# Feed-forward norm of a local-attention block: statistics per token on VectorE, factors spread by transposes, and a new written order

## The chip, the cores and the metric

The kernel runs on one core of one Trainium2 chip. The metric is the device time of one execution in microseconds (us), where smaller is better. The kernel before takes 2536.26 us, the median of three runs that lie between 2534.42 and 2536.99.

The core has engines that run side by side, each through its own instructions strictly in their order: TensorE (PE in the profile; its weight loads are shown as PEld), VectorE (DVE), ScalarE (ACT), GpSimd (POOL) and SyncE (SP), which issues DMA transfers. They wait for one another through semaphores. Matrix results land in the memory called PSUM; everything else lives in SBUF.

## The reference

One sequence of 2048 tokens with 128 features passes through four blocks, each added to its input: an oscillator recurrence with a gate, a mixture of eight experts, causal attention with 16 heads, and a stack of six layers of local attention and feed-forward. All is float32. The change lies in the last block, called stage 4:

```python
for i in range(6):
    x = attn_layer(shift_tokens(x), Wqkv[i], q_scale[i], k_scale[i], Wo[i]) + x
    x = ffn_layer(shift_tokens(x), ln_g[i], ln_b[i], W1[i], b1[i], W2[i], b2[i]) + x

def ffn_layer(x, g, bln, W1, b1, W2, b2):
    mu = x.mean(-1, keepdims=True)
    var = ((x - mu) ** 2).mean(-1, keepdims=True)
    xn = (x - mu) / jnp.sqrt(var + 1e-05) * g + bln
    hg = xn @ W1 + b1
    a, gate = jnp.split(hg, 2, -1)
    return a * jax.nn.gelu(gate, approximate=False) @ W2 + b2
```

`attn_layer` makes queries, keys and values for 16 heads of 64, normalises queries and keys to length one, rotates them, and lets each token see its own window of 32 and the one before. `shift_tokens` moves the second half of the features by one token. `ffn_layer` has 341 gated columns.

## The kernel before, in words

Stage 4 keeps the activations transposed: features on the 128 partitions, tokens along the free axis, in two SBUF tensors, `s4[0]` (input of a layer's attention) and `s4[1]` (after attention, input of its feed-forward). Attention works on tiles of 128 tokens: 16 tiles per layer, 96 in all. The feed-forward works on groups of four tiles (512 tokens): 24 groups in all.

The work of a tile is cut into some fifty named steps, that of a group into some twenty. A list named `steps`, written out by hand in the source, gives each step a place and a lag. A loop over `i` goes through the whole list each time and issues the step for tile `i - lag`; a group's step is issued only when `i - lag` is a multiple of four. So the list is the order in which every engine gets its instructions, and since engines don't reorder, it decides what waits behind what. One pass through the list is called an iteration below; four iterations carry four tiles and one group.

The steps that matter here, with the engine in brackets:

- `ps00`, `ps01`, `ps10`, `ps11` (PE): queries (ps0) and keys (ps1) in halves of 512 columns. `sq`, `ra`, `rb` read them: squares (ACT) and the two rotation products (DVE). `ss` (DVE) sums the squares, `rn` (POOL) takes the power -1/2, `rs` (POOL) adds the rotation products, `kn` (POOL) scales the keys. `tab` (POOL) makes the rotation table of the next tile.
- `pt1`, `pt0` (PE): eight transposes each of keys and queries; `kT`, `qT` (ACT) copy them out of PSUM; `ca` (POOL) carries the last window of keys into the next tile.
- `pv0`, `pv1` (PE): values; `vt` (ACT) copies them; `vw` (SP) spreads them over windows by 16 DMAs.
- `sc0` to `sc3` (PE): scores, in small tiles of 64 rows of the array; `sm` adds the mask, `mx` takes the row maximum (DVE), `nb` (POOL) scales it, `ex` (ACT) takes 16 exponentials, `su`, `nr` (DVE) sum and divide, `ptp` (PE) transposes, `pT` (ACT) copies.
- `po0` to `po3` (PE): weights times values, again in small 64-row tiles; `oT` (ACT) copies; `px0` to `px3` (PE, every other tile) multiply by Wo in tiles of 64 rows; `s` (DVE) adds the residual into `s4[1]`.
- the group's steps: the norm (`pm` to `xcn`), then for each of three column chunks `ph`, `ge`, `act` (PE, ACT with Gelu, DVE) and `py` (PE), and `s2` (DVE), which writes the next layer's `s4[0]`. In the last layer `st` transposes and stores the output.

The norm before works without leaving the transposed form. `pm` multiplies by a constant matrix of 1/128, which leaves the mean in every partition; `xc` subtracts it; `xsq` squares on ScalarE; `pvar` multiplies the squares by a column of 1/128, with one output column per 128 tokens; `fvar` adds epsilon and `fr` takes the power -1/2; `prb` spreads the factor over the partitions by four matrix products with the identity; `xcn` multiplies by factor and gain. The norm's bias is folded into the feed-forward's bias once a layer (`bias`, tile name `pbias`).

All matrix results of stage 4 take their place in one PSUM pool, `big`, of four buffers of two banks each. A step that needs a buffer waits until the steps that read its former content are done.

Of the kernel before, what the change touches and what calls it, by code (L numbers as in the profile page):

```python
# [11 lines left out]
F32 = mybir.dt.float32  # L12
BF16 = mybir.dt.bfloat16
I32 = mybir.dt.int32
AF = mybir.ActivationFunctionType
ALU = mybir.AluOpType
# [3 lines left out]
P = 128  # L20
T = 2048
NT = T // P
G = 4
NG = NT // G
GW = G * P
EPS = 1e-5
# [12 lines left out]
NPAIR = HEADS // 2  # L39
WIN = 32  # L40
# [53 lines left out]
class Kernel:  # L94
# [825 lines left out]
    def stage4(self, x3T, out):  # L920
        nc, tc, a = self.nc, self.tc, self.a
        with ExitStack() as ctx:
            self.pools4.append(ctx.enter_context(tc.tile_pool(name="s4w1", bufs=1)))
            const = ctx.enter_context(tc.tile_pool(name="s4c", bufs=1))
            pool = ctx.enter_context(tc.tile_pool(name="s4", bufs=2))
# [9 lines left out]
            carry = const.tile([P, 1], F32, name="carry")  # L935
# [30 lines left out]
            def big(name):  # L966
                return psum.tile([P, 2, 512], F32, name=name, tag="big")
# [108 lines left out]
            def qT(t):  # L1076
                st[t]["qT"] = work("qT", [P, NPAIR, P])
                act.copy(st[t]["qT"], st[t].pop(("pt", 0)))

            def kT(t):  # L1080
                if t % NT == 0:
                    st[t]["kT"] = pool3.tile([P, NPAIR, WIN + P], F32, name="kT")
                    gps.memset(st[t]["kT"][:, :, 0:WIN], 0.0)
                act.copy(st[t]["kT"][:, :, WIN:], st[t].pop(("pt", 1)))

            def ca(t):
                if t % NT + 1 < NT:
                    st[t + 1]["kT"] = pool3.tile([P, NPAIR, WIN + P], F32, name="kT")
                    gps.tensor_scalar_mul(st[t + 1]["kT"][:, :, 0:WIN], st[t]["kT"][:, :, P:], carry)

            def sc(t, i):
                q, k = st[t]["qT"], st[t]["kT"]
# [102 lines left out]
                        dve.tensor_tensor(new, old, x[rows], ALU.add)  # L1195


            def pm(g):
                ff[g]["x"] = s4[1][:, g % NG * GW : (g % NG + 1) * GW]
                ff[g]["pm"] = big("pm")[:, 0]  # L1200
                pe.matmul(ff[g]["pm"], lhsT=mean_w, rhs=ff[g]["x"], start=True, stop=True)

            def xc(g):
                ff[g]["xc"] = pool.tile([P, GW], F32, name="xc")
                dve.tensor_tensor(ff[g]["xc"], ff[g].pop("x"), ff[g].pop("pm"), ALU.subtract)

            def xsq(g):
                ff[g]["sq"] = pool.tile([P, GW], F32, name="xsq", tag="ff")
                act.activation(ff[g]["sq"], ff[g]["xc"], AF.Square)

            def pvar(g):
                sq = ff[g].pop("sq")
                ff[g]["var"] = big("pvar")[:, 0, 0:G]
                for j in range(G):
                    pe.matmul(
                        ff[g]["var"][:, j : j + 1], lhsT=sq[:, j * P : (j + 1) * P], rhs=mean_w[:, 0:1],
                        start=True, stop=True,
                    )

            def fvar(g):  # L1220
                ff[g]["r"] = pool.tile([P, G], F32, name="fvar")
                dve.tensor_scalar_add(ff[g]["r"], ff[g].pop("var"), EPS)

            def fr(g):
                gps.tensor_tensor(ff[g]["r"], ff[g]["r"], self.mhalf[:, 0:G], ALU.pow)

            def prb(g):
                r = ff[g].pop("r")
                ff[g]["prb"] = big("prb")[:, 0]
                for j in range(G):  # L1230
                    pe.matmul(
                        ff[g]["prb"][:, j * P : (j + 1) * P], lhsT=r[:, j : j + 1].to_broadcast([P, P]), rhs=self.ident,
                        start=True, stop=True,
                    )


            def xcn(g):
                x = ff[g]["xc"]
                dve.scalar_tensor_tensor(x, x, vec[:, g // NG, 0:1], ff[g].pop("prb"), ALU.mult, ALU.mult)

            def bias(l):
                w1, vc = self.w4[l][1], vec[:, l]
# [77 lines left out]
            for n in range(4):  # L1320
                for name, f in dict(sc=sc, po=po, px=px).items():
                    tiles[f"{name}{n}"] = of(f, n)
            groups = dict(pm=pm, xc=xc, xsq=xsq, pvar=pvar, fvar=fvar, fr=fr, prb=prb, xcn=xcn, s2=s2, st=store)
            for n in range(3):
                for name, f in dict(ge=ge, act=gated, py=py).items():
                    groups[f"{name}{n}"] = of(f, n)
# [3 lines left out]


            steps = [
                ("ps00", 0), ("po1", 4), ("fr", 10), ("po2", 4), ("ss1", 1), ("pt1", 2), ("ps01", 0), ("po3", 4),
                ("ss0", 1), ("kT", 2), ("s2", 15), ("sq0", 0), ("pv0", 2), ("oT", 4), ("pv1", 2), ("su", 3),
                ("sc0", 2), ("ra0", 0), ("rb0", 0), ("vt", 2), ("sc1", 2), ("sc2", 2), ("ph10", 11), ("ge0", 13),
                ("ph20", 13), ("pt0", 1), ("sc3", 2), ("ph11", 11), ("rs1", 1), ("vw", 2), ("py0", 14),
                ("act0", 13), ("qT", 1), ("nr", 3), ("sm", 2), ("mx", 2), ("rn", 1), ("ph21", 13), ("xsq", 9),
                ("ps10", 0), ("ge1", 11), ("ps11", 0), ("ptp", 3), ("py1", 14), ("st", 15), ("ph00", 12), ("nb", 2),
                ("sq1", 0), ("px0", 4), ("ge2", 13), ("ph01", 12), ("px1", 4), ("act1", 11), ("kn", 1), ("pT", 3),
                ("prb", 10), ("py2", 14), ("ra1", 0), ("px2", 4), ("px3", 4), ("pm", 8), ("ex", 2), ("act2", 13),  # L1340
                ("pvar", 9), ("ca", 2), ("rb1", 0), ("xc", 8), ("xcn", 10), ("fvar", 9), ("s", 4), ("tab", -1),
                ("po0", 3), ("rs0", 0),
            ]
            last = DEPTH * NT
            self.wo4 = {}
# [114 lines left out]
```

## Time and profile before

| | us |
|---|---|
| median of three runs | 2536.26 |
| the profiled execution's own time | 2534.71 |
| its span, first to last instruction | 2533.0 |
| PE busy in the span | 2423.0 (96%) |
| DVE busy | 1844.1 (73%) |
| ACT busy | 1728.4 (68%) |
| POOL busy | 1471.4 (58%) |
| stage 4, from its first `ps` at 846.25 to the end | 1687 |

Busy time is the union of an engine's instructions. The groups of the profile name what an instruction writes and reads (`sc<-kT,qT`), its shape, how many there were, their busy time together and the mean duration of one, and then the idle time of the engine before them with what ended it. Durations of matrix instructions overlap, so what one costs on PE is read from the timeline, as the distance between the starts of two runs. In the timeline a line is a run of equal instructions: start, length, engine, what it does, and how many. Every float32 matrix product appears as two instructions, a transpose as one. All stage 4 instructions carry line 66, a helper's, so they are told apart by the tensors' names. Rows written `SP` and `SPq` are the DMA issuing engine.

### The profile page before, as it was taken

The page shows a single profiled execution, that of the slowest core. Times are in us where ns is not written, and L with a number is a line of the kernel's source. Part 1 is how long each engine was busy: PE and PEld are TensorE (multiplying, and loading weights), DVE is VectorE, ACT ScalarE, POOL GpSimd, SP SyncE. Part 2 cuts the span into 40 slices and gives each one's busy share as a digit, 9 for nine tenths or more (in the row PEclk, how much of TensorE's full clock was granted, in tenths as well). Part 3 has the DMA queues.
Part 4 walks back from the last instruction along what each step waited for, and adds up shares of the span by engine and source line. Part 5 has one row for each costly group of instructions (what it writes and reads, how often), then busy time and mean ns, then how long its engine had stood idle before and what let it go on. Part 6 is the DMA issues. An engine that isn't in the chain of part 4 may idle for free.

```text
span 2533.0 us, 87720 instructions
## 1 busy us (share of the span) xinstructions
PE 2423.0 (96%) x38312; PEld 1441.2 (57%) x38312; DVE 1844.1 (73%) x2519; ACT 1728.4 (68%) x3233; POOL 1471.4 (58%) x1007
## 2 busy tenths in 40 slices
PE   5689999999999799999999999999999999999997
PEld 3663333333334466666666666666666666666665
DVE  7667765467653488887888778877888778878874
ACT  3323455634556377887888878887888788888884
POOL 3210000100001699888888878887888888888880
PEclk8889999989999899999999999999999999999999
DMA  2000000000000422233223322242223322222221
GB/s 79 1 1 1 1 1 1 1 1 2 1 1 1 103 70 71 68 90 77 70 70 78 93 62 70 66 101 66 72 67 91 76 70 70 67 60 64 65 68 38
DMA packets 100157, 130.13 MB, mean 51 GB/s; under 512 B 26553, under 2 KB 47681, under 8 KB 99777
## 3 DMA queue, kind: packets, MB, share of 16 engines
q1 hardware_dynamic: 99196, 124.07, 19.8%
q8 instruction: 304, 4.98, 0.9%
q14 instruction: 77, 0.62, 0.1%
q10 hardware_dynamic: 580, 0.46, 0.1%
HBM read 23.50 MB, written 1.05 MB: 10 GB/s over the span
## 4 chain that ended last, share of the span: by engine, by line
PE 90%; DVE 4%; ACT 3%; POOL 1%; issue 1%; DMA 0%; ACTq 0%; DVEq 0%; POOLq 0%
PE sc L66 21%; PE ps L66 14%; PE po L66 9%; PE pt L66 7%; PE pv L66 7%; PE px L66 7%; PE av L66 6%; PE ph L66 5%; PE py L66 4%; PE ptp L66 3%; PE prb L66 1%; PE pvar L66 1%; PE pm L66 1%; ACT ex L66 1%; DVE kT L66 1%
## 5 line engine op out<-in xcount | busy, mean ns | idle before, releaser
L66 POOL TENSOR_TENSOR rn<-ss,mhalf 128x32 f32<-128x32 f32 x96 | 524.2, 5460 | 8.0
L66 ACT ACTIVATE sm<-sm,mx,rn 128x64 f32<-128x64 f32 x1536 | 519.8, 429 | 3.7 <-POOL mx L66 3.0
L66 DVE TENSOR_REDUCE mx<-sc 128x1 f32<-128x512 f32 (+3 forms) x640 | 353.5, 604 | 222.3 <-PE sc L66 220.9
L66 ACT ACTIVATE ex<-sc 128x512 f32<-128x512 f32 (+3 forms) x640 | 306.1, 537 | 281.5 <-PE sc L66 280.4
L66 POOL TENSOR_TENSOR rot_a<-rot_a,rot_b 128x1024 f32<-128x1024 f32 x192 | 449.9, 2361 | 5.7 <-DVE rot_b L66 5.7
L66 PE MATMUL sc<-kT,qT 64*32 64x64 f32 (+2 forms) x13568 | 442.0, 259 | 8.6 <-ACT qT L66 7.8
L66 PE MATMUL ps<-wqkv,s 128*128 128x512 f32 x768 | 395.3, 619 | 2.0 <-DVE s L66 1.6
L66 POOL TENSOR_SCALAR_AFFINE_SELECT ex<-ex 128x512 f32<-128x512 f32 x64 | 40.6, 635 | 576.0 <-ACT ex L66 560.2
L66 PE MATMUL sc<-qT,kT 32*128 32x512 f32 (+3 forms) x1280 | 339.1, 581 | 4.0 <-DVE qT L66 2.1
L66 DVE TENSOR_TENSOR rot_a<-ps,tab 128x1024 f32<-128x1024 f32 x192 | 234.8, 1223 | 127.1 <-ACT sq L66 122.0
L66 PEld LDWEIGHTS sc<-kT,qT 64*32 64x32 f32 (+1 forms) x13568 | 219.5, 113 | 188.6 <-issue 108.7
L66 PEld LDWEIGHTS po<-pT,vw 64*64 64x64 f32 x12288 | 210.5, 135 | 184.9 <-issue 175.6
L66 ACT ACTIVATE sq<-ps 128x1024 f32<-128x1024 f32 x192 | 196.5, 1023 | 134.3 <-PE ps L66 97.1
L66 PE MATMUL po<-pT,vw 64*64 64x32 f32 x12288 | 242.1, 222 | 4.6 <-ACT pT L66 4.2
L66 DVE TENSOR_TENSOR rot_b<-ps,tab 128x1024 f32<-128x1024 f32 x192 | 232.9, 1213 | 0.0
L66 DVE TENSOR_REDUCE ss<-sq 128x16 f32<-128x1024 f32 x192 | 224.6, 1211 | 1.1
L66 PE MATMUL pt<-ident,rot_a 128*128 128x128 f32 x1536 | 211.4, 281 | 11.6 <-POOL rot_a L66 11.5
L66 PEld LDWEIGHTS pt<-ident,rot_a 128*128 128x128 f32 x1536 | 170.8, 142 | 46.4 <-issue 23.7
L66 PE MATMUL pv<-wqkv,s 128*128 128x512 f32 x384 | 190.6, 619 | 0.0
L66 PE MATMUL px<-oT,wo 64*128 64x128 f32 x3072 | 185.8, 276 | 0.8 <-DVE ot L66 0.8
L66 POOL TENSOR_TENSOR rot_a<-rot_a,rn 128x1024 f32<-128x1024 f32 x96 | 182.6, 1902 | 0.1
L66 PEld LDWEIGHTS px<-oT,wo 64*128 64x128 f32 x3072 | 176.6, 189 | 9.0 <-issue 4.5
(212 smaller groups left out, 3481.8 us busy)
## 6 DMA issues: line engine op xcount, KB each, us to landing
vw<-vt SPq DMA_DIRECT2D x1524, 64.0 KB, 2.0
wqkv<-in_L_ffn_Wqkv SPq DMA_DIRECT2D x18, 512.0 KB, 5.5
wo<-in_L_ffn_Wo SPq DMA_DIRECT2D x24, 256.0 KB, 6.0
w<-in_L_ffn_W SPq DMA_DIRECT2D x6, 341.0 KB, 3.6
x<-in_L_attn_hidden_states SPq DMA_DIRECT2D x4, 256.0 KB
out<-ot SPq DMA_DIRECT2D x4, 256.0 KB, 2.3
rot<-in_rot SPq DMA_DIRECT2D x1, 960.0 KB
w<-in_L_ffn_W SPq DMA_DIRECT2D x12, 64.0 KB, 4.9
```

What stands on the lines that cost most here:

```text
L66: return self._tc.keep_in_program_order(call(*args, **kw))
```

## The change

The norm of the feed-forward is computed another way, and the list `steps` is replaced by another one.

The new norm: `xt` transposes the group's 512 tokens of `s4[1]` by four transposes into PSUM, so that tokens lie on the partitions. `xs` lets VectorE take mean and variance of each token (for each 128 tokens a statistics instruction and one that aggregates it) and adds epsilon. `fr` on GpSimd takes the power -1/2 and makes minus mean times factor. `prb` spreads both over the partitions by eight transposes of broadcast columns. `xcn` computes x times gain times factor, and adds gain times the second row, in two VectorE instructions; `xc` is now written there. `pm`, `xc`, `xsq`, `pvar` and `fvar` are gone as steps.

The new list has other places and lags for nearly all steps. `kT`'s tile is now allocated through a helper, `keys`, by whichever of `ca` and `kT` comes first.

```diff
--- before.py
+++ after.py
@@ -1077,16 +1077,20 @@
                 st[t]["qT"] = work("qT", [P, NPAIR, P])
                 act.copy(st[t]["qT"], st[t].pop(("pt", 0)))
 
+
+            def keys(t):
+                if "kT" not in st[t]:
+                    st[t]["kT"] = pool3.tile([P, NPAIR, WIN + P], F32, name="kT")
+                return st[t]["kT"]
+
             def kT(t):
                 if t % NT == 0:
-                    st[t]["kT"] = pool3.tile([P, NPAIR, WIN + P], F32, name="kT")
-                    gps.memset(st[t]["kT"][:, :, 0:WIN], 0.0)
-                act.copy(st[t]["kT"][:, :, WIN:], st[t].pop(("pt", 1)))
+                    gps.memset(keys(t)[:, :, 0:WIN], 0.0)
+                act.copy(keys(t)[:, :, WIN:], st[t].pop(("pt", 1)))
 
             def ca(t):
                 if t % NT + 1 < NT:
-                    st[t + 1]["kT"] = pool3.tile([P, NPAIR, WIN + P], F32, name="kT")
-                    gps.tensor_scalar_mul(st[t + 1]["kT"][:, :, 0:WIN], st[t]["kT"][:, :, P:], carry)
+                    gps.tensor_scalar_mul(keys(t + 1)[:, :, 0:WIN], st[t]["kT"][:, :, P:], carry)
 
             def sc(t, i):
                 q, k = st[t]["qT"], st[t]["kT"]
@@ -1195,48 +1199,45 @@
                         dve.tensor_tensor(new, old, x[rows], ALU.add)
 
 
-            def pm(g):
+
+            def xt(g):
                 ff[g]["x"] = s4[1][:, g % NG * GW : (g % NG + 1) * GW]
-                ff[g]["pm"] = big("pm")[:, 0]
-                pe.matmul(ff[g]["pm"], lhsT=mean_w, rhs=ff[g]["x"], start=True, stop=True)
-
-            def xc(g):
-                ff[g]["xc"] = pool.tile([P, GW], F32, name="xc")
-                dve.tensor_tensor(ff[g]["xc"], ff[g].pop("x"), ff[g].pop("pm"), ALU.subtract)
-
-            def xsq(g):
-                ff[g]["sq"] = pool.tile([P, GW], F32, name="xsq", tag="ff")
-                act.activation(ff[g]["sq"], ff[g]["xc"], AF.Square)
-
-            def pvar(g):
-                sq = ff[g].pop("sq")
-                ff[g]["var"] = big("pvar")[:, 0, 0:G]
+                ff[g]["xt"] = big("xt")[:, 0]
                 for j in range(G):
-                    pe.matmul(
-                        ff[g]["var"][:, j : j + 1], lhsT=sq[:, j * P : (j + 1) * P], rhs=mean_w[:, 0:1],
-                        start=True, stop=True,
-                    )
-
-            def fvar(g):
-                ff[g]["r"] = pool.tile([P, G], F32, name="fvar")
-                dve.tensor_scalar_add(ff[g]["r"], ff[g].pop("var"), EPS)
+                    cols = slice(j * P, (j + 1) * P)
+                    pe.transpose(ff[g]["xt"][:, cols], ff[g]["x"][:, cols], self.ident)
+
+            def xs(g):
+                x = ff[g].pop("xt")
+                mv = ff[g]["mv"] = pool.tile([P, G, 2], F32, name="fmv")
+                for j in range(G):
+                    sx = pool.tile([P, 6], F32, name="fst")
+                    dve.bn_stats(sx, x[:, j * P : (j + 1) * P])
+                    dve.bn_aggr(mv[:, j, :], sx)
+                dve.tensor_scalar_add(mv[:, :, 1], mv[:, :, 1], EPS)
 
             def fr(g):
-                gps.tensor_tensor(ff[g]["r"], ff[g]["r"], self.mhalf[:, 0:G], ALU.pow)
+                mv, r = ff[g].pop("mv"), pool.tile([P, 2, G], F32, name="fvar")
+                gps.tensor_tensor(r[:, 0], mv[:, :, 1], self.mhalf[:, 0:G], ALU.pow)
+                gps.tensor_scalar_mul(r[:, 1], mv[:, :, 0], -1.0)
+                gps.tensor_tensor(r[:, 1], r[:, 1], r[:, 0], ALU.mult)
+                ff[g]["r"] = r
 
             def prb(g):
                 r = ff[g].pop("r")
-                ff[g]["prb"] = big("prb")[:, 0]
-                for j in range(G):
-                    pe.matmul(
-                        ff[g]["prb"][:, j * P : (j + 1) * P], lhsT=r[:, j : j + 1].to_broadcast([P, P]), rhs=self.ident,
-                        start=True, stop=True,
-                    )
+                ff[g]["prb"] = big("prb")
+                for i in range(2):
+                    for j in range(G):
+                        pe.transpose(
+                            ff[g]["prb"][:, i, j * P : (j + 1) * P], r[:, i, j : j + 1].to_broadcast([P, P]), self.ident
+                        )
 
 
             def xcn(g):
-                x = ff[g]["xc"]
-                dve.scalar_tensor_tensor(x, x, vec[:, g // NG, 0:1], ff[g].pop("prb"), ALU.mult, ALU.mult)
+                x = ff[g]["xc"] = pool.tile([P, GW], F32, name="xc")
+                p_, by = ff[g].pop("prb"), vec[:, g // NG, 0:1]
+                dve.scalar_tensor_tensor(x, ff[g].pop("x"), by, p_[:, 0], ALU.mult, ALU.mult)
+                dve.scalar_tensor_tensor(x, p_[:, 1], by, x, ALU.mult, ALU.add)
 
             def bias(l):
                 w1, vc = self.w4[l][1], vec[:, l]
@@ -1320,7 +1321,7 @@
             for n in range(4):
                 for name, f in dict(sc=sc, po=po, px=px).items():
                     tiles[f"{name}{n}"] = of(f, n)
-            groups = dict(pm=pm, xc=xc, xsq=xsq, pvar=pvar, fvar=fvar, fr=fr, prb=prb, xcn=xcn, s2=s2, st=store)
+            groups = dict(xt=xt, xs=xs, fr=fr, prb=prb, xcn=xcn, s2=s2, st=store)
             for n in range(3):
                 for name, f in dict(ge=ge, act=gated, py=py).items():
                     groups[f"{name}{n}"] = of(f, n)
@@ -1330,16 +1331,15 @@
 
 
             steps = [
-                ("ps00", 0), ("po1", 4), ("fr", 10), ("po2", 4), ("ss1", 1), ("pt1", 2), ("ps01", 0), ("po3", 4),
-                ("ss0", 1), ("kT", 2), ("s2", 15), ("sq0", 0), ("pv0", 2), ("oT", 4), ("pv1", 2), ("su", 3),
-                ("sc0", 2), ("ra0", 0), ("rb0", 0), ("vt", 2), ("sc1", 2), ("sc2", 2), ("ph10", 11), ("ge0", 13),
-                ("ph20", 13), ("pt0", 1), ("sc3", 2), ("ph11", 11), ("rs1", 1), ("vw", 2), ("py0", 14),
-                ("act0", 13), ("qT", 1), ("nr", 3), ("sm", 2), ("mx", 2), ("rn", 1), ("ph21", 13), ("xsq", 9),
-                ("ps10", 0), ("ge1", 11), ("ps11", 0), ("ptp", 3), ("py1", 14), ("st", 15), ("ph00", 12), ("nb", 2),
-                ("sq1", 0), ("px0", 4), ("ge2", 13), ("ph01", 12), ("px1", 4), ("act1", 11), ("kn", 1), ("pT", 3),
-                ("prb", 10), ("py2", 14), ("ra1", 0), ("px2", 4), ("px3", 4), ("pm", 8), ("ex", 2), ("act2", 13),
-                ("pvar", 9), ("ca", 2), ("rb1", 0), ("xc", 8), ("xcn", 10), ("fvar", 9), ("s", 4), ("tab", -1),
-                ("po0", 3), ("rs0", 0),
+                ("ps00", 0), ("pT", 4), ("ps01", 0), ("ph21", 14), ("mx", 3), ("py0", 15), ("xcn", 11), ("rn", 2),
+                ("py1", 15), ("nb", 3), ("py2", 15), ("sq0", 0), ("ra1", 1), ("po0", 4), ("po1", 4), ("ge2", 14),
+                ("ex", 3), ("rb1", 1), ("rb0", 0), ("po2", 4), ("kn", 2), ("s2", 15), ("tab", -1), ("px0", 5),
+                ("px1", 5), ("st", 15), ("px2", 5), ("ra0", 0), ("ph00", 13), ("xt", 9), ("act2", 14), ("xs", 9),
+                ("ss1", 1), ("px3", 5), ("po3", 4), ("s", 5), ("pt1", 2), ("kT", 2), ("vw", 3), ("ph10", 11),
+                ("ph01", 13), ("pt0", 1), ("ph11", 11), ("ca", 3), ("ss0", 1), ("oT", 4), ("pv0", 2), ("qT", 1),
+                ("pv1", 2), ("su", 3), ("sc0", 2), ("rs1", 1), ("sc1", 2), ("nr", 3), ("vt", 2), ("sc2", 2),
+                ("sc3", 2), ("ge1", 11), ("ge0", 13), ("sm", 2), ("ps10", 0), ("act0", 13), ("ps11", 0),
+                ("prb", 10), ("fr", 9), ("act1", 11), ("ph20", 13), ("ptp", 3), ("sq1", 0), ("rs0", 0),
             ]
             last = DEPTH * NT
             self.wo4 = {}
```

## The prediction

> **What bounds the kernel now.** I read the page first, then busy time by stretches of stage 4, then the waits, then the order of matrix instructions.
>
> ```profile
> PE 2423.0 (96%) x38312; PEld 1441.2 (57%) x38312; DVE 1844.1 (73%) x2519; ACT 1728.4 (68%) x3233; POOL 1471.4 (58%) x1007
> ...
> PE 90%; DVE 4%; ACT 3%; POOL 1%; issue 1%; DMA 0%; ACTq 0%; DVEq 0%; POOLq 0%
> ```
>
> PE makes up 90% of the chain that ended last. By stretches (length; PE, PEld, DVE, ACT, POOL busy; granted clock; DMA share, GB/s):
>
> ```profile
> 1400.00:1700.00 300.00, 300.00 (x5804) 195.93 (x5804) 241.53 (x251) 242.13 (x430) 250.65 (x148) 0.99 0.30 74
> ...
> 1464.00:1471.00 7.00, 7.00 (x77) 4.27 (x76) 3.67 (x6) 2.78 (x7) 6.92 (x5) 0.53 0.01 2
> ```
>
> In 300 us PE has no gap; DVE, ACT and POOL are free for a sixth of it. The second row is a stretch at half clock, used below. The waits of 860 to 2480 us say the same:
>
> ```profile
> POOL mx L66 <- DVE mx L66: 215.4, 81, 5.6
> ...
> PE pt L66 <- POOL rot_a L66: 8.8, 2, 4.9
> ```
>
> The others wait often; PE's longest sum is 8.8 us. The starts of `pm` confirm it: most groups follow each other at exactly 67.77 us. So stage 4 costs what its PE instructions cost, and that is read from the timeline (start, length, run):
>
> ```profile
> 1600.97 1.05 PE L66 MATMUL pvar<-mean_w,xsq 128*128 128x1 f32 x8
> 1601.95 0.67 PE L66 MATMUL po<-pT,vw 64*64 64x32 f32 x32
> 1602.55 1.12 PE L66 MATMUL ps<-wqkv,s 128*128 128x512 f32 x2
> 1603.60 1.14 PE L66 MATMUL po<-pT,vw 64*64 64x32 f32 x64
> 1604.67 1.09 PE L66 MATMUL pt<-ident,rot_a 128*128 128x128 f32 x8
> 1605.60 1.02 PE L66 MATMUL ps<-wqkv,s 128*128 128x512 f32 x2
> 1606.55 0.67 PE L66 MATMUL po<-pT,vw 64*64 64x32 f32 x32
> 1607.15 1.98 PE L66 MATMUL pv<-wqkv,s 128*128 128x512 f32 x4
> 1609.07 1.17 PE L66 MATMUL sc<-kT,qT 64*32 64x64 f32 x96
> 1610.17 1.09 PE L66 MATMUL pt<-ident,rot_a 128*128 128x128 f32 x8
> 1611.19 0.45 PE L66 MATMUL sc<-kT,qT 64*32 64x64 f32 x32
> 1611.57 1.13 PE L66 MATMUL py<-act,w 128*128 128x512 f32 x2
> 1612.54 1.88 PE L66 MATMUL ps<-wqkv,s 128*128 128x512 f32 x4
> 1614.25 1.04 PE L66 MATMUL ptp<-ident,sm 128*128 128x128 f32 x8
> ```
>
> A run costs the distance to the next start. Four `ps` among full-size runs cost 1.71, so 0.43 each; four `pv` between `po` and `sc` cost 1.92. A visit to the small 64-row tiles thus delays the full run before it by 0.09 and the one after it by 0.10 (single starts show which). The visit pays a third part: 64 `po` cost 1.07, 32 cost 0.60, so 0.13 to 0.14 is fixed. One visit costs **0.33**, or 0.29 where transposes follow (late by 0.06). The 0.11 of one transpose is eight `ptp` in 0.87.
>
> **The change on PE, per group of four iterations.** *Work removed:* `pm` 0.95, `pvar` 0.98, old `prb` 0.89, together 2.82. *Added:* `xt`, four transposes giving way to `po`, 3 x 0.11 + 0.20 = 0.53; new `prb`, eight, 0.88. Net -1.4.
>
> *Visits removed:* before, each iteration goes to `po` three times and `sc` twice; with the one `px` run that `pvar` parts from `po` that is 21. After, `sc` is whole (4 visits), and `po` with `px` is one block in iterations 0, 2 and 3 and two in iteration 1 (counting iterations by i modulo 4): 9. Twelve fewer at 0.31 are 3.7. Against it speaks the Trainium skill, "TensorEngine Tiling (Array Packing)", Key Properties: changing the tiling mode, not just the tile, drains TensorE; the new order goes from `po` (64*64) to `px` (64*128) and back inside a block, in iterations 0 and 2. By the rule all four changes cost. The nearest row: `px` gives way to `po` 0.10 late; `po` to `px` is nowhere in the trace, bounded by 0 and the 0.14 with which `po` gives way to full runs. I take the upper: 4 changes 0.48 against 0.10 before, so -3.7 becomes -3.3. Were they free, another 0.5 would go.
>
> Laid end to end in the new order with these costs, PE needs 15.35, 14.79, 17.08 and 15.74 in iterations 0 to 3, together **63.0**, against 67.8 (-1.4 and -3.3 agree).
>
> **The other engines, and the waits.** Their sums per group: DVE 55.9 today from its groups; `xc` (0.69) goes, a second product (0.74) comes, and `xs` comes for `fvar` (0.16). The groups of the first 860 us, before stage 4, have the same statistics (busy, mean ns | idle before):
>
> ```profile
> L66 DVE BATCH_NORM_STATS2 ln_st<-x 128x6 f32<-128x128 f32 x48 | 12.7, 265 | 0.0
> ...
> L66 DVE BATCH_NORM_AGGREGATE ln_mv<-ln_st 128x2 f32<-128x6 f32 x48 | 8.7, 182 | 1.7
> ```
>
> Pairs start 0.39 apart there, so `xs` costs 4 x 0.39 + 0.3 = 1.9, DVE 57.7. There the source is SBUF, here PSUM: the mask addition reads PSUM in 1.22 and the division SBUF in 1.22, so I take no surcharge (bounds 0 and twice, 1.0). ACT loses `xsq` (0.63); four table loads of 1.28 stay, as the Gelu steps again touch two spells between exponentials. POOL: 57.0 plus `fr` 1.04 + two small operations of 0.2. All stay under 63, but with 5 to 9 to spare, so order decides. I walked the new order through one cycle by hand, with the durations above, ACT copies 0.92 apart, 16 exponentials 5.42, `rn` 5.46, `rs` 2.36, 0.1 to 0.2 per hand-over, and the built program's buffer waits:
>
> - *Iteration 1.* The second half of `ps` ends at 1.8; `sq0` runs 2.0 to 2.95, the exponentials to 8.4, `kT` to 9.4. PE is through `po`, `ph00`, `xt`, `pt1` (5.4, just held by `ra0`, 5.5), `ph01` and `pt0` at 8.1. `pv0` takes the buffer that `kT` empties: it waits until 9.45, **1.4**. Behind it stand `pv`, `sc`, `ps1`, `ptp` and the next tile.
> - *Iterations 0 and 2* pay a table load, so `kT` ends at 10.7 and 11.3, but there `pv0` takes `px`'s buffer (free once `s` has read it, 8.1 and 8.9, wanted 9.5 and 10.4), and `sc` starts at 11.3 and 12.2. No wait. The nearest miss: `ps10` wants `qT`'s buffer at 12.66, free at 12.65.
> - *Iteration 3*: `py` comes early, `pv0` is wanted at 9.9 and `kT` done at 9.4. `s2` (6.0) and `xcn` precede `ph10` (7.3). No wait.
> - *DVE*: `mx` of an iteration ends between -0.8 and +1.0 about its start, before `nb` is wanted at 2.9. `xs` ends at 7.3 in iteration 1; its cover is the wait for `kT`: 0.4 more for each statistics instruction would delay `pt0` to where PE notices.
> - *POOL*: `kn` ends by 5.0 at the latest, `pt1` wants it at 5.4 to 8.6; `tab` now waits for `rb1` (2.8), behind it `ca` (done by 5.5; `sc0` wants it at 9.9 or later), `rs1`, `fr`, `rs0`, which `pt0` wants an iteration later.
> - *SP*: `vw` issues 16 DMAs, 0.63 apart (10.2), landing 2.0 later. Released by `vt` at 12 to 14, they are in by 9.5 of the next iteration; `po` wants them at 1.8 of the one after, and the loads of the next layer stand behind them as before. Cost nothing.
>
> So a group takes 63.0 + 1.4 = **64.4**, 3.4 less. Steady stage 4 runs from 899 to 2467, 23 groups: **-79**. Filling and draining keep their number of iterations; I take nothing.
>
> *Clock.* The half-clock row shown above comes right after `pvar`, 32 `po` and `pbias` (2.3 us of one-column products in 2.9). Two of five such crossings fell to half clock; those groups took 72.1 where the others took 69.0, so 3.1 each. Without `pvar` one-column work halves: 0 to 6 us gained, I take 3. Could the new 1.4 wait bring such drops? The Trainium skill, "TensorE: Matmul & The Clock Gate", HAM oscillation, asks only that idle gaps stay below about 3.4 us: by it, no cost. The row shows a drop with no PE gap at all; at its rate, 2 in 5, 23 waits would cost 28. I go by the rule, because `pvar` alone, 1.0 of thin work in each group, never did it.
>
> Sum: 2534.7 (profiled time) - 79 - 3 = 2453; the median stood 1.6 above the profiled execution: **2455**.
>
> **Rivals.**
> - *No wait at `pv0`* (the exponentials earlier, or buffers falling otherwise): 4.8 a group, all 6 of the clock: 2536 - 110 - 6 = 2420. Against: the chain `ps01` to `kT` is fixed by rows.
> - *The fewer visits don't pay*: they come back as waits, `pv0` waiting for `kT` everywhere: iteration 0 then takes 16.6, 1 16.2, 2 18.0, 3 15.7, 66.5 in all, and only the removed work's 1.3 to 1.4 remain: 2536 - 32 = 2504. For it: margins of 0.0 to 0.5 in several places.
> - *Slower by the clock*: each group's wait at `pv0`, amid transposes, brings half-clock stretches. At 3.1 each, 1.1 per group eat the 3.4; two per group give 2455 + 143 = 2598, 1.2 or 1.3 about 2540 to 2550. For it: drops without a gap. Against: 1.4 is short.
> - *Nothing moves*: PE's gain is lost wholly to waits not seen here, 2536.
>
> **How the numbers follow.** Likeliest 2455, chance 0.55, its own range 2436 to 2476 (0.5 a group either way for the unknown change `po` to `px` and the tight margins, the clock's 0 to 6). No wait 0.10, visits not paid 0.20, nothing moves 0.05, slower 0.10. From the no-wait case to just past the unpaid visits, 2418 to 2508, leaves out about 0.15. A difference of 0.2% is about what a measurement of this kernel can tell. Faster 0.85, same 0.05, slower 0.10.
>
> **What would show it.** Groups of 64.4 (distance of `xt` starts); `sc` as runs of 128 instructions at 1.35; idle PE time before `pv`, some 1.4 once per group, ended by ACT `kT`; `xs` pairs 0.39 apart; granted clock near 1.00. Wrong: waits of PE on `pt`, `ps` or `po` in each iteration, `po` to `px` dearer than 0.14, or clock drops in every group.

## The result, and the profile after

The changed kernel takes 2513.43 us, the median of four runs between 2507.70 and 2516.99. Beside it the kernel before took 2536.01. The ratio is 0.9909, with a 95% interval of 0.9890 to 0.9929. The prediction was 2455, with a range of 2418 to 2508: the direction was right, the size was not, and the time lies just above the range.

On the page of the changed kernel, busy time and chain of work:

```profile
PE 2352.1 (94%) x38168; PEld 1445.5 (58%) x38168; DVE 1880.5 (75%) x2711; ACT 1710.1 (68%) x3209; POOL 1488.0 (59%) x1055
...
PE 86%; DVE 4%; ACT 4%; issue 2%; POOL 2%; SPq 1%; DMA 0%; ACTq 0%; DVEq 0%; POOLq 0%
```

TensorE lost 71 us of busy time (2423.0 before), close to the 79 that I forecast for the groups. But the span only fell by 20, from 2533.0 to 2513.0. So most of the work went away, and holes came in its place. The waits of 860 to 2480 us on TensorE (what it was about to do, what ended the wait; us in total, times, longest) show which:

```profile
PE sc L66 <- issue: 16.7, 15, 2.7
PE po L66 <- issue: 11.3, 9, 1.6
PE pt L66 <- POOL rot_a L66: 10.8, 3, 7.0
PE pv L66 <- ACT kT L66: 10.1, 17, 0.7
PE px L66 <- issue: 3.6, 6, 1.2
```

Before, the longest sum here was 8.8 us. Three of the five rows say "issue": TensorE stood still, although the profile shows no engine and no transfer for which it waited. The timeline shows where (start, length, run; in brackets the idle time before it):

```profile
1504.05 1.92 PE L66 MATMUL po<-pT,vw 64*64 64x32 f32 x92
1507.57 0.31 PE L66 MATMUL po<-pT,vw 64*64 64x32 f32 x4 [1.60 <-issue]
...
1577.51 1.98 PE L66 MATMUL pv<-wqkv,s 128*128 128x512 f32 x4 [0.61 <-ACT kT L66]
...
1628.96 1.20 PE L66 MATMUL sc<-kT,qT 64*32 64x64 f32 x101
1631.67 0.44 PE L66 MATMUL sc<-kT,qT 64*32 64x64 f32 x27 [1.50 <-issue]
```

A run of 96 `po` stops after 92 for 1.6 us, a run of 128 `sc` after 101 for 1.5 us. (These numbers count matrix instructions, two for each float32 product. Where I or an expectation speak of 96 or 128 products, these instructions are meant.) In the middle of a run of equal instructions nothing new is needed, so this is hardly a wait for data. I call these stops **pauses**: 0.3 us or more from the start of one instruction to the start of the next within one run of `sc`, `po` or `px`, counted from 980 to 2430 us. The kernel before has none. The kernel after has 28, which together last 33 us.

They have one thing in common. If TensorE's instructions (weight loads, products and its semaphore instructions) are numbered from the start of the trace, there are 77,540, or 302.9 times 256. The page of after lists the transfers that bring instructions in the row `q8 instruction: 303, 4.96, 0.8%`: 303 packets of 16,384 bytes, one for each 256. In the kernel after 25 of the 28 pauses stand at instruction 193 of a block of 256, whatever runs there. (The other three lie between 2420 and 2425, at a granted clock of 0.67 for the stretch 2418 to 2426.) Each of the 25 ends 1.2 to 1.6 us after a packet has landed: in block k + 1 of the program it is the k-th packet on record. The same limit holds where nothing stops. In all 3177 blocks from 980 to 2430 us of this document's fourteen kernels, no instruction 193 starts less than 1.19 us after the landing of that packet. In the kernel before 6 of 225 blocks come within 1.65 us of it, in the kernel after 36 of 228. So in a pause TensorE waits for its own program.

Groups follow each other (distance of `xt` starts) at 64.2 at the least and 66.45 in the median, where 67.77 was the rule before. The mean over the 22 whole groups fell from 68.15 to 66.91.

### The profile page after: what moved, and what is told of

Its sections match the earlier page's. It is cut to its first block, busy times and chain, and to the rows that moved or that the text cites. A ratio compares the mean times of both kernels' runs of the same rounds, so it can differ in the third digit from the quotient of the medians.

```text
span 2513.0 us, 87693 instructions
## 1 busy us (share of the span) xinstructions
PE 2352.1 (94%) x38168; PEld 1445.5 (58%) x38168; DVE 1880.5 (75%) x2711; ACT 1710.1 (68%) x3209; POOL 1488.0 (59%) x1055
## 3 DMA queue, kind: packets, MB, share of 16 engines
q8 instruction: 303, 4.96, 0.8%
## 4 chain that ended last, share of the span: by engine, by line
PE 86%; DVE 4%; ACT 4%; issue 2%; POOL 2%; SPq 1%; DMA 0%; ACTq 0%; DVEq 0%; POOLq 0%
PE sc L66 21%; PE ps L66 13%; PE po L66 9%; PE px L66 8%; PE pv L66 6%; PE pt L66 6%; PE av L66 6%; PE ph L66 5%; PE py L66 4%; PE ptp L66 3%; SPq L66 1%; PE prb L66 1%; ACT sm L66 1%; POOL rot_a L66 1%; ACT ex L66 1%
## 5 line engine op out<-in xcount | busy, mean ns | idle before, releaser
L66 PE MATMUL sc<-kT,qT 64*32 64x64 f32 (+2 forms) x13568 | 430.2, 259 | 28.3 <-issue 16.7
L66 PE MATMUL ps<-wqkv,s 128*128 128x512 f32 x768 | 373.4, 610 | 4.6 <-DVE vec L66 2.4
L66 ACT ACTIVATE sq<-ps 128x1024 f32<-128x1024 f32 x192 | 196.7, 1024 | 212.2 <-issue 109.5
L66 PE MATMUL po<-pT,vw 64*64 64x32 f32 x12288 | 235.6, 221 | 14.7 <-issue 11.3
L66 DVE TENSOR_TENSOR rot_a<-ps,tab 128x1024 f32<-128x1024 f32 x192 | 233.7, 1217 | 14.4 <-ACT sq L66 13.7
L66 PE MATMUL pt<-ident,rot_a 128*128 128x128 f32 x1536 | 200.2, 280 | 13.8 <-POOL rot_a L66 13.5
L66 PEld LDWEIGHTS ps<-wqkv,s 128*128 128x128 f32 x768 | 132.1, 192 | 109.0 <-issue 96.7
L66 PE MATMUL pv<-wqkv,s 128*128 128x512 f32 x384 | 183.7, 601 | 10.2 <-ACT kT L66 10.1
```

What stands on the lines that cost most here:

```text
L66: return self._tc.keep_in_program_order(call(*args, **kw))
```

## The experiments

All kernels with their median time, the ratio to the kernel before that ran with them, the time of the one execution that was profiled, and the mean group and the pauses (number, us together) in it. The profiled execution can lie up to 11 us from the median, so groups, pauses and waits belong with its time:

| kernel | us | ratio (95%) | profiled | mean group | pauses |
|---|---|---|---|---|---|
| before | 2536.01 | | 2534.71 | 68.15 | 0 |
| after | 2513.43 | 0.9909 (0.9890 to 0.9929) | 2514.68 | 66.91 | 28, 33 |
| v1_norm_only | 2511.61 | 0.9897 (0.9873 to 0.9920) | 2510.03 | 66.99 | 1, 0.4 |
| v2_order_only | 2562.85 | 1.0087 (1.0060 to 1.0113) | 2565.61 | 69.12 | 29, 37 |
| v3_sc_whole | 2558.15 | 1.0071 (1.0040 to 1.0102) | 2558.15 | 69.14 | 7, 6 |
| v9_sc_whole_ptp | 2632.96 | 1.0372 (1.0336 to 1.0407) | 2626.63 | 71.80 | 12, 16 |
| v5_pT_early | 2500.83 | 0.9844 (0.9816 to 0.9872) | 2491.38 | 66.10 | 24, 22 |
| v8_sc_parted | 2541.35 | 1.0023 (1.0002 to 1.0044) | 2551.58 | 68.05 | 14, 15 |
| v12_vw_once | 2493.62 | 0.9814 (0.9771 to 0.9856) | 2499.68 | 65.87 | 14, 19 |
| v13_vw_unread | 2492.35 | 0.9825 (0.9795 to 0.9855) | 2494.05 | 66.05 | 15, 21 |
| v10_po_joined | 2501.57 | 0.9859 (0.9818 to 0.9900) | 2498.23 | 66.50 | 3, 1 |
| v11_po_px_joined | 2507.77 | 0.9877 (0.9836 to 0.9918) | 2508.32 | 66.59 | 3, 3 |
| v14_po_all | 2533.39 | 0.9981 (0.9958 to 1.0004) | 2533.32 | 67.98 | 20, 25 |
| v15_po_joined_eps | 2491.03 | 0.9815 (0.9787 to 0.9843) | 2479.66 | 65.86 | 4, 4 |

### The two halves of the change

`v1_norm_only` is the new norm in the old written order:

```diff
-("pm", 8) ... ("xsq", 9) ... ("xc", 8) ... ("pvar", 9) ... ("fvar", 9)
+("xt", 8) ... ("xs", 8)          # all other places as before
```

> The new norm in the old order: xt, xs stand where pm and xc stood; xsq, pvar, fvar are gone; all else as before. Theory A (instruction supply: whole runs of small tiles outrun the delivery of PE's instructions) and the prediction's sum agree here: the old order has no whole runs, PE stays gapless, so the removed work counts in full, 1.4 us a group, 23 groups, -32: about 2504. Rival (the norm itself is what disappoints, through VectorE or PSUM buffers): no better than the changed kernel, 2513 or more.

Measured: 2511.61 beside 2538.76 for the kernel before in the same batch, 27 less. The norm's -1.4 per group times 23 were 32. So this part of the sum is nearly right, and it alone is as fast as the whole change. The most frequent group fell by 1.04, from 67.77 to 66.73: the work that went is the forecast 1.4, and most of the difference came back in the iteration with `xt`, where `pv` starts 0.10 later and `pt0` another 0.23.

`v2_order_only` is the old norm in the new order:

```diff
-("xt", 9) ... ("xs", 9) ... ("fr", 9)
+("pm", 9) ... ("xc", 9) ... ("vt", 2), ("xsq", 9) ... ("pvar", 9), ("ptp", 3), ("fvar", 9) ... ("nb", 3), ("fr", 10)
```

> The old norm in the new order: pm where xt stood, xc where xs stood, xsq behind vt, pvar ahead of ptp, fvar behind ptp, fr an iteration later behind nb. The prediction's sum: visits -3.3 and wait +1.4 leave -1.9 a group: 2536 - 44 = 2492. Theory A: pauses in whole runs (1.5 a group), po's late start (0.6), the wait at pv0 (0.6) and the end of the stage take nearly all: changed kernel plus 32, so 2540 to 2548.

Measured: 2562.85, 24 us **slower** than before, and slower than both expectations. Its waits on TensorE:

```profile
PE sc L66 <- issue: 18.0, 14, 2.3
PE po L66 <- issue: 10.5, 7, 2.1
...
PE px L66 <- issue: 4.8, 5, 1.5
```

The pauses came with the order, not with the norm: 37 us of them, and 33 in the kernel after. The forecast gives this half 44 us of gain (1.9 in each of 23 groups), and the pauses alone take most of it. Its trace also has 41 us at half clock between 960 and 2480, where the kernel before has 14; at the 3.1 us that the prediction read from each 6.8 of them, the 27 more are an estimated 12 us of loss. The rest was not followed up.

### Joining `sc` alone, in the old order

`v3_sc_whole` is the kernel before with all 128 `sc` products together:

```diff
-("sc2", 2), ("ph10", 11), ("ge0", 13), ("ph20", 13), ("pt0", 1), ("sc3", 2), ("ph11", 11)
+("sc2", 2), ("sc3", 2), ("ph10", 11), ("ge0", 13), ("ph20", 13), ("pt0", 1), ("ph11", 11)
```

> The kernel before with one edit: sc3 moved up behind sc2, so that the scores are one run of 128 matrix instructions; pt0 (and ph10, ph20 where they come) follow it. One visit of 0.33 fewer per tile. The prediction's price: -0.33 x 92 = -30, 2506, and no gap inside sc. Theory A: pauses of about 1.3 inside sc, near its end, in one tile of six, as in the changed kernel (19 us in all), none before: net -8 to -14, 2522 to 2528.

Measured: 2558.15, 19 us slower, where both theories had it faster. The saving itself is there: in an iteration without `ph`, from the start of `sc` to the start of `ptp` (`sc`, `pt`, `ps`), TensorE needs 4.06 us instead of 4.33. But its waits have a new first row:

```profile
PE ps L66 <- ACT qT L66: 18.7, 64, 0.3
...
PE sc L66 <- issue: 4.6, 7, 1.7
```

`ps` takes the PSUM buffer that `qT` empties. `qT` copies what `pt0` has transposed, and `pt0` now stands behind 32 more `sc` products. So everything from `pt0` to the next `ps` moved back by a third of a microsecond, and in three iterations of four the visit's gain of 0.27 was lost and as much again paid.

`v9_sc_whole_ptp` asks whether the visit is worth its price once that wait is covered:

```diff
# v3_sc_whole, and:
-("ps10", 0), ("ge1", 11), ("ps11", 0), ("ptp", 3)
+("ptp", 3), ("ps10", 0), ("ge1", 11), ("ps11", 0)
```

> v3_sc_whole (the kernel before with sc3 directly behind sc2; 2558), with the transposes ptp moved from behind the second ps1 product run to ahead of the first, so that the copy qT has 0.9 us more before ps1 takes its buffer. If the visit was worth its 0.3 and v3 lost only by that wait: the wait of ps for qT (62 times, 18.1 us) is gone, 92 visits at 0.29 are 27 saved, some 6 of pauses inside sc stay: 2538 - 27 + 6 = 2517. If a whole sc costs by itself, because what it holds up is released later: 2550 to 2560 with another wait in the place of qT's.

Measured: 2632.96, much slower than any expectation, and 98 us slower than the kernel before in its batch. The wait for `qT` is gone, and a larger one stands in its place, which holds half of that:

```profile
PE ptp L66 <- DVE sm L66: 48.7, 42, 1.9
PE sc L66 <- issue: 12.9, 11, 2.2
```

`ptp` needs VectorE's division of the former tile, which isn't ready that early; behind `ptp` stand both `ps1`. So the test says nothing on the price of a visit. It says that the old order had no slack there. The other half of the loss was not assigned.

### `po`'s slow start

In the kernel after, 96 `po` take 1.86 us where they follow `ps` (iterations 0 and 1), and 1.53 where they follow `ph`. The 0.33 lies in the 8th to 15th instruction, where the waits for `vw`'s DMAs stand: 0.03 to 0.076 each in the median, where the same places take 0.007 (every fourth 0.038) in v5_pT_early below. `pT`, which `po` also needs, is done 0.5 us before `po` starts. `v5_pT_early` takes that last condition away by doing `ptp` and `pT` some microseconds sooner, ahead of the second half of `ps1`:

```diff
-("ps00", 0), ("pT", 4), ("ps01", 0)
-("ps10", 0), ("act0", 13), ("ps11", 0) ... ("ph20", 13), ("ptp", 3), ("sq1", 0)
+("ps00", 0), ("ps01", 0)
+("ps10", 0), ("act0", 13), ("ptp", 3), ("pT", 3), ("ps11", 0) ... ("ph20", 13), ("sq1", 0)
```

> The changed kernel with ptp moved between ps10 and ps11, and pT behind it at the end of the iteration (lag 3), so that pT is done 1 us earlier against po0. Theory B (po's start is slow because PE reaches its waits for pT and for vw only when pT is just done): the 0.3 at po's start in iterations 0 and 1 goes, 0.6 a group, -13: about 2500. If po's slow start has another cause: no change, 2513.

Measured: 2500.83, as expected, and 96 `po` behind `ps` take 1.53 in the median. Shown next to each other, the run of after and one of this kernel:

```profile
1570.13 1.91 PE L66 MATMUL po<-pT,vw 64*64 64x32 f32 x96
```

```profile
1559.72 1.60 PE L66 MATMUL po<-pT,vw 64*64 64x32 f32 x96
```

So the cause of the slow start is shown. That the whole time fits so well is in part luck: the pauses shrank too (24, 22 us instead of 28, 33), and a new small wait of 12.9 us came, `pt` for VectorE's `rot_a`, 25 times.

### What the pauses depend on

My theory was that a dense run eats its 256 instructions faster than the next packet comes. `v8_sc_parted` breaks the run of `sc` in two:

```diff
# v5_pT_early, and:
-("pv0", 2), ("qT", 1), ("pv1", 2), ("su", 3), ("sc0", 2), ("rs1", 1), ("sc1", 2), ("nr", 3), ("vt", 2), ("sc2", 2)
+("pv0", 2), ("qT", 1), ("su", 3), ("sc0", 2), ("rs1", 1), ("sc1", 2), ("nr", 3), ("pv1", 2), ("vt", 2), ("sc2", 2)
```

> v5_pT_early (2500.8 us), with the second half of pv moved between sc1 and sc2, so that no more than 64 score products stand together. Supply theory (a packet of 256 TensorE instructions is asked for late and is there 2.3 to 2.9 us later; a whole sc run eats 256 instructions in 1.4): the runs of v5 that stand still inside sc (11 times, 14.4 us) nearly vanish, none over 0.6; one more visit to the small tiles in each of 92 iterations costs 0.29 each, +27; sum 2500.8 + 27 - 11 = 2517. If the pauses have nothing to do with how dense the run is, they stay at 14 us and the time is 2528. If a visit costs nothing in this order, only the pauses go: 2490.

Measured: 2541.35. The waits of v8_sc_parted on TensorE:

```profile
PE ps L66 <- ACT vt L66: 11.6, 37, 0.3
PE sc L66 <- issue: 9.8, 9, 2.5
PE sc L66 <- ACT kT L66: 7.9, 15, 2.1
```

The pauses in `sc` fell only from 14.4 to 9.8 us, with single ones of up to 2.5, though no run is longer than 64. So the length of the run is **not** what decides alone, and the theory fell in that form. (The pauses in `po` and `px`, whose runs weren't touched, fell from 13 to 6.) The time also went past every expectation. A new wait of 11.6 us, of `ps` for the buffer that `vt` empties later now, is part of it; the rest was not assigned.

All of its 14 pauses are at instruction 193 of a block again. Over all kernels it is 167 of 174. So the packet must be there by a fixed place, and the question becomes when it sets out. Numbering from the start of the block with its own number (the k-th packet, the k-th block), a packet starts to move at instruction 220 in the median before, and 193 of the following block (449 in the same count) is the place where TensorE stops. In the kernel after the median is 267, so packets start 47 instructions later, and 182 are left to the stop instead of 229. The medians go with the pauses: 217 to 238 in the kernels with 0 to 7 pauses, 239 to 267 in those with 14 and more, so the two ranges touch; only v9_sc_whole_ptp has 12 at 232.

What makes packets start late? `v12_vw_once` and `v13_vw_unread` ask for the transfers of `vw`. In the first they are left out for 15 tiles of 16; in the second they run into a tile that isn't read.

```diff
# v12_vw_once: the kernel after, and in vw(t)
+if t % NT:
+    st[t]["vw"] = st[t - 1]["vw"]
+    return
# v13_vw_unread: the kernel after, and in vw(t)
+if t % NT:
+    vw = const.tile([P, NWIN, NPAIR, HD], F32, name="vwd")
+    st[t]["vw"] = st[t - 1]["vw"]
+else:
+    vw = st[t]["vw"] = const.tile([P, NWIN, NPAIR, HD], F32, name="vwl")
```

> The kernel after, but vw is spread only for the first tile of each layer and all 16 tiles of the layer use it (15 of 16 tiles' values are left out): 16 DMAs per iteration and the waits of po for them go, the order of TensorE's instructions stays. It asks why instruction packets come late in the new order. If they are held up by vw's transfers, or TensorE's own look-ahead is by the many DMA waits at po: the 33 to 36 us of pauses fall below 8 and po's slow start (14 us) goes, 2513 - 28 - 14 = 2471. If the pauses belong to the order of the instructions alone: they stay near 30 us, only po's start goes, 2499. If po's slow start isn't vw's waits either: 2510.

> The kernel after; vw's 16 DMAs per iteration run as they do there, but into a tile that nobody reads, and po reads the tile of the layer's first 128 tokens (the values of the other 15 tiles are left out). The traffic stays, po's waits for it go. v12_vw_once, without both, took 2493.6 and had 14 pauses of 18.9 us, only 2 of them in po and px, where the kernel after has 15 there. If the traffic held up the instruction packets: 25 to 30 pauses again, some 12 of them in po and px, 33 us, time 2505 to 2510. If the waits did, by keeping TensorE from looking ahead: about 14 pauses as in v12_vw_once, and 2490 to 2497. In both cases po's slow start (96 po in 1.86 instead of 1.53) is gone.

Measured: 2493.62 and 2492.35, with 14 pauses of 19 us and 15 of 21 us. The first lies between its expectations, the second is the one in which the waits are behind the pauses. The waits of v13_vw_unread:

```profile
PE pv L66 <- ACT kT L66: 20.8, 22, 1.7
PE sc L66 <- issue: 17.0, 14, 2.1
...
PE po L66 <- issue: 4.3, 2, 2.4
...
PE px L66 <- issue: 0.8, 1, 0.8
```

Without `po`'s waits for the DMAs, the 16 pauses in `po` and `px` of the kernel after (three of them at half clock) became 2, and the slow start of `po` is gone (1.53 everywhere). Since it makes no difference whether the transfers run, it is the waits and not the traffic. How the waits delay the packets is not shown. It is not by the slow start: v5_pT_early has none and still 13 pauses in `po` and `px`. (Without the waits TensorE also has 720 instructions fewer, 0.9%, so the blocks' borders fall elsewhere.) The pauses in `sc` stayed at 12 and 13. Some 11 us of what was freed went into the wait of `pv` for `kT`, which grew from 10.1 to 20.8.

### Fewer visits to the small tiles, with the new norm

`v10_po_joined` joins 96 `po` in the old order:

```diff
# v1_norm_only, and:
-("ps00", 0), ("po1", 4), ("fr", 10), ("po2", 4), ("ss1", 1)
+("po1", 4), ("fr", 10), ("po2", 4), ("ps00", 0), ("ss1", 1)
```

> v1_norm_only (the new norm in the old order; 2511.6 us), with the first half of ps0 moved from between po0 and po1 to behind po2: 96 po products stand together, one visit to the small tiles fewer in each iteration. By the visits' price: -0.31 x 92 = -28, 2483. By the supply theory: 192 instructions in 1.5 us lie at the limit, a few short pauses inside po, no more than 5 us: 2483 to 2489. If visits saved come back as waits as in v3_sc_whole: 2505 to 2535, with a wait of TensorE of 0.3 or more in most iterations.

Measured: 2501.57, 10 less than v1_norm_only instead of 28, with three pauses. The most frequent group fell from 66.73 to 66.11, by half of the price of four visits. The price itself is right: from the first `po` of an iteration to `po3`, with the same work between, TensorE needs 4.31 us instead of 4.60. The other half is in the waits, 14.8 us in 22 groups:

```profile
PE pt L66 <- DVE rot_b L66: 8.2, 20, 0.7
PE pv L66 <- ACT kT L66: 6.6, 21, 0.4
```

`v11_po_px_joined` was to take three more visits per group:

```diff
# v10_po_joined, and:
-("px0", 4) ... ("ph01", 12), ("px1", 4) ... ("prb", 10), ("py2", 14) ... ("px3", 4), ("xt", 8)
+("ph01", 12), ("py2", 14), ("prb", 10), ("xt", 8), ("px0", 4) ... ("px1", 4) ... ("px3", 4)
```

> v10_po_joined, and in addition ph01, py2, prb and xt moved ahead of px, so that px and po are one block: three visits fewer per group, 3 x 0.31 x 23 = 21. By price v10's time less 21, 2462 if v10 gives 2483; by the supply theory the block px, po0 to po2 takes 320 instructions in 5.4 us, the last 192 in 1.5, so pauses no more than in v10. If the saving comes back as waits: no faster than v10.

Measured: 2507.77, with groups of 66.1 as in v10_po_joined. The expectation was mistaken: in the timeline of v10_po_joined `px` already stands as one run of 64 with `po` behind it. It is issued every second iteration, and the four steps come in the others. There was no visit to save, so this run mostly shows how far two kernels of the same TensorE work differ here, 6 us, which is within the noise of four runs each.

`v14_po_all` puts the last 32 `po` beside the other 96:

```diff
# v10_po_joined, and:
-("po2", 4), ("ps00", 0), ("ss1", 1), ("pt1", 2), ("ps01", 0), ("po3", 4)
+("po2", 4), ("po3", 4), ("ps00", 0), ("ss1", 1), ("pt1", 2), ("ps01", 0)
```

> v10_po_joined (2501.6 us; the new norm in the old order with ps00 behind po2), with po3 moved up beside po2, so that all 128 po products stand together: one visit to the small tiles fewer in each iteration. By the visits' price: -0.31 x 92 = -28, 2473. As in v10_po_joined, where half of the price came back as waits of pv for kT and of pt for rot_b: 2487. If it all comes back, or the run of 256 instructions pauses often: 2500 or more.

Measured: 2533.39, 32 us slower than v10_po_joined; the last of the three expectations came true:

```profile
PE po L66 <- issue: 13.7, 10, 1.8
PE pv L66 <- DVE s L66: 9.3, 18, 0.5
...
PE sc L66 <- issue: 8.3, 10, 2.0
```

Twenty pauses came back, 11 of them in `sc`, although `sc` stands as in v10_po_joined, which had two there. Stops at instruction 193 in other runs (`pt`, `ph`, `ps`), which my count leaves out, add 11.5 us here. So a pause needn't lie in the run that was joined.

`v15_po_joined_eps` takes on the wait for `rot_b`. In v10_po_joined one small instruction is out of proportion (GpSimd's timeline, and VectorE's beside it):

```profile
1431.50 4.68 POOL L66 TENSOR_TENSOR rot_a<-rot_a,rot_b 128x1024 f32<-128x1024 f32 x2
...
1432.00 1.88 DVE L66 TENSOR_SCALAR fmv<-fmv 128x4 f32<-128x4 f32 x1
```

The addition of epsilon to four numbers per partition takes 1.89 in the mean, and it ends when the first of GpSimd's two additions ends (at 1433.85). In 22 of 23 groups it is so, each time 0.03 behind GpSimd. In the kernel after it takes 0.18. The edit lets GpSimd add epsilon:

```diff
 def xs(g):
-    dve.tensor_scalar_add(mv[:, :, 1], mv[:, :, 1], EPS)
 def fr(g):
+    gps.tensor_scalar_add(mv[:, :, 1], mv[:, :, 1], EPS)
     gps.tensor_tensor(r[:, 0], mv[:, :, 1], self.mhalf[:, 0:G], ALU.pow)
```

> v10_po_joined (2501.6 us) with epsilon added by GpSimd in fr instead of by VectorE in xs. In v10_po_joined that small VectorE addition takes 1.89 us (0.18 in the kernel after), ending with a GpSimd addition that runs beside it. Without it VectorE is 1.9 earlier once per group: the wait of pt for rot_b (20 times, 8.2 us) goes, the wait of pv for kT (6.6 us) stays: 2493. If the 1.9 is off the path, 2501.

Measured: 2491.03, as expected, and the fastest of the kernels that compute everything. It beats the kernel before by 1.6 to 2.1%. Against v10_po_joined the ratios' intervals overlap a little, but the most frequent group fell from 66.11 to 65.60, which in 22 groups is 11 us. The page, and the waits on TensorE:

```profile
PE 2357.7 (95%) x38168; PEld 1413.0 (57%) x38168; DVE 1876.9 (76%) x2687; ACT 1707.5 (69%) x3209; POOL 1489.9 (60%) x1079
```

```profile
PE pt L66 <- POOL rot_a L66: 8.8, 2, 4.9
PE pv L66 <- ACT kT L66: 6.3, 20, 0.3
```

The row of `rot_b` is gone from the top. In the profiled executions TensorE is busy 6 us longer than in the kernel after, and the span is 35 us shorter (22 between the medians): fewer holes beat less work.

## Why the prediction was wrong, step by step

*What bounds the kernel* held: TensorE is 86% of the chain after.

*Work removed and added, -1.4 per group:* right as prices. `xt` took 0.530 (predicted 0.53), the new `prb` 0.873 (0.88). v1_norm_only gained 27 of 32, with 1.04 of the 1.4 in its most frequent group.

*Prices of single runs:* right but for one. `po` gives way to `px` 0.149 late, the upper bound that I took (0.14), where instructions inside its run start 0.015 apart in the mean. That agrees with the rule of the Trainium skill, "TensorEngine Tiling (Array Packing)", Key Properties, that a change of mode drains TensorE. A whole `sc` costs 1.41 instead of the 1.34 to 1.35 that I set: 0.3 per group, 6.5 us in 22. Laid end to end without waits, the order came to 63.0, and its shortest group was 64.2, against the 64.4 predicted with the wait.

*Wait of `pv0` for `kT`, 1.4 once a group:* the right wait at the right place, but 17 times with 10.1 us together, 0.6 each. `kT` is done at 9.13 us after the iteration's first `ps` (I had 9.4), and `pv0` starts at 9.19 in nearly every group (I had 9.45). But TensorE comes to it at 8.4 instead of 8.1, because of `po`'s slow start of 0.33; so here the slow start only takes the place of the wait. In v12_vw_once and v13_vw_unread, without it, the wait is 20.8 us. Stops of TensorE ahead of it took away all or most of it in only four groups.

*"No wait" in other places, and visits that pay their 0.31:* **this is the step that failed.** I priced TensorE's program as if its instructions were always at hand and its waits were free once met. Against 22 groups of 64.4, and the 8.5 us above 22 x 67.77 that the kernel before has too, the measured 1472.1 us are 47 more. Of these the three "issue" rows are 32; `po`'s slow start 14 (42 runs of 0.33); `sc` 6.5; the smaller `pv0` wait gives 20 or 21 back. That leaves some 15. Some 8 of them lie in the last of the 22 groups, which takes 71.7, with 10.2 us of it at half clock; the kernel before has 65.3 there. I can't assign the remaining 7 to one row.

*Filling and draining, nothing:* wrong by 7 us. From the first `xt` on record (969.4, against 968.0 for the first `pm`) and after the last group counted (71.4 us, against 65.5).

*The clock, -3:* did not come. The two half-clock stretches of 6.8 us before, at 1464 and 1740, are gone, but between 969 and 2440 the kernel after has three others, at 1356 (3.4 us), 2407 (3.4) and 2421 (6.8): 13.6 us at half clock in both kernels. The last two are in the group of 71.7. Each of the three starts 0.5 to 1.2 us after an idle gap of TensorE of 1.2 to 1.6 us; behind the longest gap (2.7 us, at 1162) there was none. So short waits may not be free for the clock, as I had put them, but no run shows that these gaps caused the drops. v1_norm_only, also without `pvar`, has none in this stretch.

*VectorE, ACT, POOL and SP at nothing:* right for this kernel, as far as the waits show, apart from `po`'s 16 DMA waits. The statistics read PSUM in 0.27 (predicted 0.265). But it was luck for the small addition, which took 1.89 in the order of v10_po_joined.

Together: 47 in the groups, 3 of the clock (the 8.5 above still holds what the forecast took off), 3.4 for the 23rd group that I counted as steady, and 7 at the ends make 60 of the 62 us between forecast and span.

Of the rivals, "the fewer visits don't pay" (2504, chance 0.20) was nearest, and v1_norm_only (2511.61) lies near its sum. Its reason, `pv0` waiting for `kT` everywhere, was not the one.

What stays open: why packets start later in the joined orders. The waits of `po` for 16 DMAs are shown to be behind half of the pauses. For those in `sc` no cause was found: breaking up the run took away a third of their time, and joining all of `po` in the old order (v14_po_all) brought them.

## What to carry to other kernels

A saving on the busiest engine is worth its price only if what that engine waits for next is ready earlier too. For each step that a new order moves back, follow what hangs on it (the copy, the buffer that it frees, the step that takes this buffer), as with `pt0`, `qT` and `ps`. Where TensorE runs thousands of tiny products, look for idle time "issue" inside runs of equal instructions: its program arrives in blocks, and a new order can make it wait for them although no data is late. Change one thing at a time, and try the parts of a large reordering separately: here one half held the whole gain.

## What the runs showed of the hardware

- TensorE's program comes in packets of 16,384 bytes for 256 instructions. Where a packet was late, TensorE stopped at instruction 193 of a block (167 of 174 pauses), for up to 3.0 us in the kernel after and 4.0 in v12_vw_once, and went on 1.2 to 1.6 us after the packet had landed. In none of 3177 blocks did instruction 193 come less than 1.19 us after that landing.
- The `po` instructions with the DMA waits took 0.03 to 0.076 us each, 0.33 together, where TensorE reached them 0.5 us after `pT`, their other condition, was done. They cost nothing extra when `pT` had been done some microseconds earlier (v5_pT_early), nor without the DMA waits (v12_vw_once, v13_vw_unread).
- A VectorE addition over 128 x 4 numbers from SBUF to SBUF took 1.74 us (v1_norm_only) to 1.89 us (v10_po_joined) in the mean where GpSimd ran an addition over 128 x 1024 beside it, ending 0.03 us after GpSimd's in all 22 long cases of either kernel, and 0.18 where it fell at another time (the kernel after). The statistics next to it, from PSUM, took 0.27 in both.
